# Half of the four copies that place a turned attention tile are issued by GpSimd instead of SyncE

## The chip, the cores and the metric

The kernel runs on one core of a Trainium2 chip. The metric is the device time of one execution in microseconds (us). Before the change the median of three runs is 8271.41 us, the runs lie between 8253.08 and 8294.09 us.

The engines of the core are TensorE (PE in the profile, its weight loads PEld), VectorE (DVE), ScalarE (ACT), GpSimd (POOL) and SyncE (SP). SyncE computes nothing; it issues most of the transfers. SPq and POOLq are the sequencers that issue a transfer.

## The reference, cut to what matters

```python
# x: (4, 128, 64, 64) float32
x = x + deform_conv3x3(group_norm(x))          # layer 0: offsets and mask from a conv, bilinear gather
t = to_tokens(x)                               # (4, 4096, 128)
u = ln(t)
qkv = qz_ring(u.reshape(4, 4096, 16, 8) + rx)  # 16 heads of 8: cosines and their running products
s = einsum('bhsd,bhtd->bhst', q, q) / sqrt(8)  # q, k and v are the same tensor
ctx = einsum('bhst,bhtd->bhsd', softmax(s), q)
x1 = ln(u + ctx @ w_comb.T + b_comb)
t = t + ln(x1 + relu(cos(x1[..., :8]) * cos(ry) @ w1.T + b1) @ w2.T + b2)
t = t + moe_top2_of_8(ln(t))
out = from_tokens(t)
```

The attention carries most of the time: four batches, 16 heads, 4096 positions each. Queries and keys are the same tensor, so the matrix of scores of a head is symmetric, and so is its exponential. A block of exponentials that has been computed for the query chunk `sc` and the key tile `t` serves a second time, turned round, with `t` as the queries and `sc` as the keys.

## The kernel before, in words

**The attention loop.** The main loop (from L1499) goes over `steps`. A step is one key tile `t` of 128 positions for one run; a run is a batch, a group of four heads and a query chunk `sc` of 512 positions. `scores` (L1323) makes four matmuls (L1331) and two exponentials of 128x1024 on ScalarE (L1340), which give the tiles `e`. `context` (L1344) multiplies them with the values `qf` into the accumulator `acc` (L1354). The scores run up to two steps (`LAG`) ahead of the context.

**The turned tiles.** For some steps (`gives`) the block of exponentials is used a second time. `turn` (L1200) does it in three stages:

1. VectorE transposes the two `e` tiles in blocks of 32x32 into a tile `st` of 128x2048 floats (L1210, two instructions).
2. `move` (L1218) takes a tile `et` and issues four transfers (L1222). Copy `r` reads partitions 32r to 32r+31 of `st` (8 KB in each) and writes slot `r` of all 128 partitions of `et` (2 KB in each): 256 KB a copy, 1 MB a turned tile.
3. `from_turned` (L1268) makes 32 matmuls of TensorE (L1277) from `et` and the values `vt` into `acc`, in two halves of 16. It needs all four copies.

There are 704 turned tiles, so 2816 copies. Two `st` buffers (`NST`) and three `et` buffers (`NET`) are in use by turns. An `st` is free when its four copies have read it; an `et` is free when TensorE has used it.

**What sets the order.** The order of the instructions on TensorE, VectorE, SyncE and GpSimd is the order of the program text, which a planner, the class `Beside` (L65), works out as the program is written. Each engine then carries out its own list in order, and waits where a semaphore isn't there yet. The planner keeps an estimate of time for TensorE (`now`), VectorE (`dve`) and GpSimd (`pool`). Jobs beside the attention (the preparation of the next batch, the feed forward and the experts of a finished chunk, the turned tiles) are slotted in when the planner holds them ready. `later(when, emit)` writes an instruction down once the planned time `when` is past; the copies of a turned tile are written at the planned end of its transposes (L1228), or when an `et` comes free (L1234 to L1245). The matmuls of a turned tile are planned at 6.0 us after the copies (L1226).

**SyncE's list.** It holds, besides the copies of the turned tiles, nearly all other transfers: keys and values (L1302, L1304), queries (L1312, L1316), the store of a run's context (L1178), the transfers of the preparation (L729, L762, L882, L883) and of the layers behind the attention.

**GpSimd's list.** It holds the 1152 indirect gathers of the deformable convolution (`gather`, L650; three to a unit of work, up to two units ahead), 132 small powers that give the reciprocal standard deviation of the norms (`rsqrt`, L410 to L417), and 32 copies of the features (L859). The planner books a unit's three gathers with 3.9 us on `pool` and their landing 2.8 us later (`gathered`, L197), and a power with 1.1 us (`powered`, L202). The gathers end with the preparation of the last batch.

Of the kernel before, what the change touches and what calls it, by code (L numbers as in the profile page):

```python
# [229 lines left out]
def ve(n, ops=1):  # L230

    return ops * (0.17 + n / 960.0)
# [12 lines left out]
def kernel(  # L245
# [22 lines left out]
    nc = tc.nc  # L268
# [12 lines left out]
    beside = Beside()  # L281
# [918 lines left out]
    def turn(es, run, t):  # L1200
        b, g, sc = runs[run][:3]
        while len(unsent) >= NST:
            beside.flush()
            if len(unsent) >= NST:
                beside.pull("turned")
        unsent.append(run)
        st = work.tile([P, 4, 4, P], F32, tag="st", name=f"st{run}_{t}", bufs=NST)
        beside.dve = max(beside.dve, beside.now + 0.9)
        for pr in range(2):
            nc.vector.transpose(  # L1210
                out=st[:, :, 2 * pr : 2 * pr + 2, :].rearrange("p o h (q j) -> p o (h q) j", j=32),
                in_=es[pr].rearrange("p h (q o i) -> p o (h q) i", o=4, i=32),
            )
            beside.dve += ve(1024)

        outstanding[run] += 1

        def move():  # L1218
            unsent.remove(run)
            e = work.tile([P, 4, 4, P], F32, tag="et", name=f"et{run}_{t}", bufs=NET)  # L1220
            for r in range(4):
                nc.sync.dma_start(  # L1222
                    out=e[:, r].rearrange("p h x -> p (h x)"),
                    in_=st[32 * r : 32 * (r + 1)].rearrange("p o h x -> p (o h x)"),
                )
            beside.add("turned", from_turned(run, t, e, beside.now + 6.0), -1)  # L1226

        beside.later(beside.dve, lambda: granted(move))  # L1228
# [5 lines left out]
    def granted(emit):  # L1234
        if room[0]:
            room[0] -= 1
            emit()
        else:
            asking.append(emit)
# [28 lines left out]
    def from_turned(run, t, e, landed):  # L1268

        b, _, sc = runs[run][:3]  # L1270
        kt = t % 4
        part = 1 + gifts[b][sc].index(t // 4)
        for half in range(2):
            yield need(pe=MM256, hold=None, after=landed)
            for q in (2 * half, 2 * half + 1):
                for h in range(4):
                    nc.tensor.matmul(  # L1277
                        accs[run][32 * h : 32 * (h + 1), P * kt : P * (kt + 1)],
                        lhsT=window(q, h, part),
                        rhs=e[:, :, h, 32 * q : 32 * (q + 1)],  # L1280
                        start=False, stop=False,
                    )
        outstanding[run] -= 1
        beside.later(beside.now + 0.9, returned)
# [363 lines left out]
```

## Time and profile before

| | |
|---|---|
| median of three runs | 8271.41 us (8253.08 to 8294.09) |
| the profiled execution | 8280.98 us, its span 8279.2 us |
| mean granted clock of TensorE | 0.932 of full speed |
| TensorE busy | 7100.3 us, 86% of the span |
| ScalarE busy | 6385.2 us, 77% |
| VectorE busy | 5251.0 us, 63% |
| GpSimd busy | 1630.9 us, 20% |
| copies of turned tiles (L1222), all on SyncE | 2816 |
| first and last of them | 966.2 us, 7986.3 us |
| gathers on GpSimd (L650) | 1152, the last at 6055.5 us |

All lines that are quoted come from one profiled execution. An engine is busy while one of its computing instructions runs; the issue of a transfer isn't counted. A group of instructions in the profile is given by its line, engine, operation and tiles (written<-read), then its count, then busy time and mean duration, then the idle time of the engine just before those instructions, with what ended most of it. A line of the waits names the waiting instruction, the one that it waited for, then the total in us, the number of waits and the longest one. The chain of waits is followed back from the last instruction: each step goes to what released it.

### The profile page before, as it was taken

The numbers are of one execution on the slowest core, as the hardware profiler recorded it, in microseconds if no ns is written. First come the engines' busy times: TensorE is split into PE (matmuls) and PEld (weight loads), VectorE is DVE, ScalarE is ACT, GpSimd is POOL, SyncE is SP. The second block draws the span as 40 slices with busy tenths as digits, with TensorE's granted clock in tenths as the row PEclk, the third lists the DMA queues.
The fourth block names the chain that finished last, engine by engine and source line by source line (L and its number), as shares of the span: only waits on it lengthen the run. The fifth ranks groups of instructions, "written<-read, shape, count | busy, mean of one in ns | idle before, by whom it ended". The sixth has DMA issues, their size and how long they took to land.

```text
span 8279.2 us, 196502 instructions
## 1 busy us (share of the span) xinstructions
PE 7100.3 (86%) x79896; PEld 2614.4 (32%) x79896; DVE 5251.0 (63%) x9904; ACT 6385.2 (77%) x6825; POOL 1630.9 (20%) x1327
## 2 busy tenths in 40 slices
PE   3689898989998888889898888888899998898996
PEld 2122232222333333333333333333333333333332
DVE  7666366664555777767565776666665665666555
ACT  0579898879887778778687877777788887787894
POOL 5443043421002313213000322122200000000000
PEclk6789999999999999999899999999999999999998
DMA  6777478785567788887757888887775777778641
GB/s 180 214 216 203 132 231 221 222 227 141 142 168 203 203 222 232 221 231 202 189 142 187 251 229 234 226 216 210 206 187 138 176 202 188 196 197 210 176 119 38
DMA packets 1051268, 1598.91 MB, mean 193 GB/s; under 512 B 188994, under 2 KB 418012, under 8 KB 1050364
## 3 DMA queue, kind: packets, MB, share of 16 engines
q1 hardware_dynamic: 950654, 1280.06, 59.7%
q0 software_dynamic: 92160, 302.06, 11.9%
q8 instruction: 630, 10.32, 0.5%
q10 hardware_dynamic: 7550, 4.22, 0.2%
q14 instruction: 274, 2.24, 0.1%
HBM read 612.82 MB, written 234.90 MB: 102 GB/s over the span
## 4 chain that ended last, share of the span: by engine, by line
PE 47%; DMA 23%; SPq 13%; DVE 11%; issue 4%; ACT 1%; POOL 1%; ACTq 0%; DVEq 0%; POOLq 0%
PE acc L1354 21%; DMA et<-st 17%; PE sc L1331 12%; SPq L1222 9%; PE acc L1277 6%; DVE st L1210 4%; PE conv_ps L301 2%; PE e_ps L301 2%; DVE v L670 1%; DMA sT<-smd 1%; SPq L729 1%; PE f_ps L301 1%; ACT e L1340 1%; DMA v<-tab,idx 1%; DMA smd<-tr 1%
## 5 line engine op out<-in xcount | busy, mean ns | idle before, releaser
L1340 ACT ACTIVATE e<-sc 128x1024 f32<-128x1024 f32 x6784 | 6379.0, 1058 | 1723.4 <-PE sc L1331 1512.2
L1354 PE MATMUL acc<-e,qf 128*9 128x512 f32 (+1 forms) x26368 | 3583.2, 615 | 31.8 <-DVE cu L1568 22.4
L1331 PE MATMUL sc<-qT,kT 32*128 32x512 f32 x13568 | 2136.3, 506 | 127.1 <-ACT e L1340 42.9
L1210 DVE STREAM_TRANSPOSE st<-e 128x1024 f32<-128x1024 f32 x1408 | 1666.2, 1222 | 910.2 <-DMA et<-st 633.1
L1331 PEld LDWEIGHTS sc<-qT,kT 32*128 32x128 f32 x13568 | 857.1, 186 | 3336.2 <-ACT e L1340 2822.6
L650 POOL DMA_INDIRECT v<-tab,idx x1152 | 1434.3, 1245 | 1907.5 <-DVE tr L717 1385.5
L1277 PE MATMUL acc<-et,vt 128*32 128x128 f32 x22528 | 970.4, 294 | 716.3 <-DMA et<-st 693.6
L1277 PEld LDWEIGHTS acc<-et,vt 128*32 128x32 f32 x22528 | 580.6, 115 | 1086.1 <-issue 951.2
L1354 PEld LDWEIGHTS acc<-e,qf 128*9 128x9 f32 (+1 forms) x26368 | 626.8, 93 | 566.6 <-issue 311.1
L415 POOL TENSOR_TENSOR r<-ln_t,expo 128x4 f32<-128x4 f32 x96 | 110.5, 1151 | 3246.0 <-DVE ln_t L413 3166.1
L670 DVE TENSOR_TENSOR v<-v,wt 128x1536 f32<-128x1536 f32 x384 | 666.5, 1736 | 103.4 <-DMA v<-tab,idx 103.3
L675 DVE TENSOR_TENSOR v<-v 128x768 f32<-128x768 f32 x384 | 366.7, 955 | 8.0
L717 DVE STREAM_TRANSPOSE tr<-v 128x128 f32<-128x128 f32 x1080 | 248.7, 281 | 188.8 <-DMA smd<-tr 182.5
L301 PE MATMUL conv_ps<-sT,wconv_sb 128*32 128x256 f32 x4320 | 353.9, 401 | 0.0
L1105 DVE TENSOR_TENSOR eo<-e_ps,gt 128x512 f32<-128x512 f32 x256 | 173.5, 680 | 271.3 <-PE e_ps L301 269.2
L1566 DVE COPY cu<-acc 128x512 f32<-128x512 f32 x128 | 88.3, 690 | 225.3 <-PE acc L1354 225.2
L676 DVE TENSOR_TENSOR v<-v 128x384 f32<-128x384 f32 x384 | 215.5, 561 | 13.3
L1259 DVE COPY vt<-own 128x144 f32<-128x144 f32 x96 | 22.7, 236 | 268.8 <-PE acc L1277 268.7
L859 POOL COPY fx<-rn 128x512 f32<-128x512 f32 x32 | 28.0, 874 | 765.5 <-DVE rn L858 487.4
L301 PE MATMUL f_ps<-w_sb,h 128*32 128x128 f32 x4096 | 169.1, 285 | 0.0
L415 POOL TENSOR_TENSOR rstd<-lt_t,expo 128x4 f32<-128x4 f32 x32 | 53.5, 1673 | 510.0 <-DVE lt_t L413 439.0
L301 PEld LDWEIGHTS conv_ps<-sT,wconv_sb 128*32 128x32 f32 x4320 | 105.6, 112 | 93.4 <-issue 89.6
(232 smaller groups left out, 3440.5 us busy)
## 6 DMA issues: line engine op xcount, KB each, us to landing
et<-st SPq DMA_DIRECT2D x2816, 256.0 KB
kT<-kTd SPq DMA_DIRECT2D x333, 256.0 KB
smd<-tr SPq DMA_DIRECT2D x360, 192.0 KB
sT<-smd SPq DMA_DIRECT2D x360, 192.0 KB
qT<-qTd SPq DMA_DIRECT2D x166, 256.0 KB
atd<-cu SPq DMA_DIRECT2D x128, 256.0 KB
qf<-fqd SPq DMA_DIRECT2D x333, 72.0 KB
aT<-atd SPq DMA_DIRECT2D x76, 256.0 KB
```

What stands on the lines that cost most here:

```text
L301: nc.tensor.matmul(dst[c : c + 32], lhsT=lhsT[:, c : c + 32], rhs=rhs, start=start, stop=stop)
L650: nc.gpsimd.indirect_dma_start(out=v[:, k, :], out_offset=None, in_=tab, in_offset=bass.IndirectOffsetOnAxis(ap=idx[:, j, kk : kk + 1], ax ...
L670: nc.vector.tensor_tensor(v4, v4, w12[:, :, None].to_broadcast([P, 12, C]), ALU.mult)
L675: nc.vector.tensor_tensor(v[:, :, : 2 * C], v[:, :, : 2 * C], v[:, :, 2 * C :], ALU.add)
L676: nc.vector.tensor_tensor(v[:, :, :C], v[:, :, :C], v[:, :, C : 2 * C], ALU.add)
L717: nc.vector.transpose(out=tr9[:, k, :, j % 4, :], in_=v[:, k, :C].rearrange("p (c i) -> p c i", i=32),)
L1210: nc.vector.transpose(out=st[:, :, 2 * pr : 2 * pr + 2, :].rearrange("p o h (q j) -> p o (h q) j", j=32), in_=es[pr].rearrange("p h (q o i ...
L1222: nc.sync.dma_start(out=e[:, r].rearrange("p h x -> p (h x)"), in_=st[32 * r : 32 * (r + 1)].rearrange("p o h x -> p (o h x)"),)
L1277: nc.tensor.matmul(accs[run][32 * h : 32 * (h + 1), P * kt : P * (kt + 1)], lhsT=window(q, h, part), rhs=e[:, :, h, 32 * q : 32 * (q + 1)] ...
L1331: nc.tensor.matmul(ps[i // 2][:, i % 2, :], lhsT=kT[h : h + 32, P * (t % 4) : P * (t % 4 + 1)], rhs=qT[h : h + 32, :], start=True, stop=True,)
L1340: nc.scalar.activation(e, ps[pr], AF.Exp, scale=1.0 / math.sqrt(HD))
L1354: nc.tensor.matmul(acc[32 * h : 32 * h + width, :], lhsT=lhsT, rhs=es[h // 2][:, h % 2, :], start=(t == ts[0]), stop=(t == ts[-1]),)
```

## The change

`move` writes the same four copies. Copies 0 and 1, which read partitions 0 to 63 of `st`, stay on SyncE; copies 2 and 3, which read partitions 64 to 127, go to GpSimd. They are written in the order 0, 2, 1, 3, and the planner books 2.2 us on its estimate for GpSimd for each turned tile. Nothing else is touched; source, destination and size of each copy stay.

```diff
         def move():
             unsent.remove(run)
             e = work.tile([P, 4, 4, P], F32, tag="et", name=f"et{run}_{t}", bufs=NET)
-            for r in range(4):
-                nc.sync.dma_start(
+            beside.pool = max(beside.pool, beside.now) + 2.2
+            for r in (0, 2, 1, 3):
+                (nc.gpsimd if r > 1 else nc.sync).dma_start(
                     out=e[:, r].rearrange("p h x -> p (h x)"),
                     in_=st[32 * r : 32 * (r + 1)].rearrange("p o h x -> p (o h x)"),
                 )
```

## The prediction

> **What bounds the kernel now.** I read the page's busy times first, then its chain of waits, then the groups, then the waits of TensorE and of SyncE's queue, and last the chain piece by piece.
>
> ```profile
> PE 47%; DMA 23%; SPq 13%; DVE 11%; issue 4%; ACT 1%; POOL 1%; ACTq 0%; DVEq 0%; POOLq 0%
> PE acc L1354 21%; DMA et<-st 17%; PE sc L1331 12%; SPq L1222 9%; PE acc L1277 6%; DVE st L1210 4%; PE conv_ps L301 2%; PE e_ps L301 2%; DVE v L670 1%; DMA sT<-smd 1%; SPq L729 1%; PE f_ps L301 1%; ACT e L1340 1%; DMA v<-tab,idx 1%; DMA smd<-tr 1%
> ...
> L1210 DVE STREAM_TRANSPOSE st<-e 128x1024 f32<-128x1024 f32 x1408 | 1666.2, 1222 | 910.2 <-DMA et<-st 633.1
> ...
> L650 POOL DMA_INDIRECT v<-tab,idx x1152 | 1434.3, 1245 | 1907.5 <-DVE tr L717 1385.5
> L1277 PE MATMUL acc<-et,vt 128*32 128x128 f32 x22528 | 970.4, 294 | 716.3 <-DMA et<-st 693.6
> ```
>
> The way of a turned tile holds a quarter of the chain: its copies' flight 17%, their issue by SyncE 9%. The chain also runs where TensorE has other work, so these 26% aren't the gain. What the copies cost is TensorE's idle time: 716.3 us ahead of L1277, 693.6 of them ended by a copy's landing. TensorE is idle for 1161 us in all (gaps between its matmuls, added up); most of the other 445 us lies ahead of the first turned tile and in the tail. So the copies are the one large wait of the bottleneck engine, and 716 us is the most that mending them can save. VectorE, too, waits 633.1 us for copies to have read an `st`.
>
> The last piece shows one tile:
>
> ```profile
> 6627.28 0.23 SPq L1222
> 6627.51 0.04 issue
> 6627.55 1.18 SPq L1222
> 6628.73 0.04 issue
> 6628.78 0.91 SPq L1222
> 6629.69 0.04 issue
> 6629.73 6.27 DMA et<-st
> 6636.00 0.14 issue
> 6636.14 0.65 PE acc L1277 x16
> ```
>
> Issue after issue on SyncE, then the flight, then the matmuls at once. The records of all 704 tiles say the same: the four issues take 0.63, 0.85, 1.21 and 1.41 us in the mean (4.1 us, 2816 of them 2884 us of SyncE's time); later ones take longer[...]. From the first issue to the last landing pass 8.17 us in the median (7.4 to 9.95 for eight in ten), 8.48 in the mean. In 393 tiles the matmuls begin within 0.4 us of the landing. From the transposes' end to the first issue pass 0.07 us in the median, 1.36 in the mean; the copies then stand behind others on SyncE:
>
> ```profile
> SPq L1178 <- DVE cu L1566: 859.5, 99, 41.8
> SPq L1222 <- DVE st L1210: 609.1, 326, 8.9
> SPq L1304 <- PE acc L1354: 265.5, 80, 8.4
> ```
>
> **SyncE's part.** It loses 1408 issues. Its two copies no longer stand behind two others: 0.63 + 0.85 = 1.5 us of issue, and in the few tiles with nothing else on the queues the second copy landed some 5.3 us after the first issue, with two more behind it. I put SyncE's half at 5 to 6 us. SyncE also gains 1408 x 1.3 us (the mean of the third and fourth) = 1.8 ms of free time, so L1302, L1304 and L1312 come earlier; they are no large wait of TensorE (36 and 34 us for keys and queries, in the opening), so I count nothing. SyncE's half still stands behind L1178 and L1304 as before.
>
> **GpSimd's part.** No plain transfer of GpSimd is in the trace. The nearest row is its gather, also 256 KB in 128 rows: 1.245 us each in the mean (0.94 to 2.53), 0.30 us between two. Two copies: 2 x 1.25 + 0.3 = 2.8 us. Is GpSimd free? At the transposes' end it is at work in 8% of the tiles, and the stretch of work before it gets to a new entry is 0.37 us in the mean. Then the flight: from a gather's issue to its landing pass 4.85 us in the median (at least 2.13), but those read HBM in three at a time; SyncE's fourth copy lands 3.84 us after its issue in the median, 3.5 for the quickest quarter, with three copies ahead of it in its queue. GpSimd's has one, so I take 3.5. Its half lands 0.37 + 2.8 + 3.5 = 6.7 us after the transposes. That is the later half: the tile lands 8.48 - 6.7 = 1.8 us sooner. Bounds: with 4.85 us of flight 8.0, so 0.2 to 0.5 sooner than today's median and mean; with 0.94 us an issue, no hold and 2.13 us of flight SyncE's half is the later one at some 5.3, so 3.2 sooner.
>
> **What 1.8 us is worth.** I go through TensorE's 327 waits ahead of L1277 (median 1.3 us, a tenth over 5.2) and cut each by the lead: 1.0 us sooner saves 275 us, 1.5 saves 362, 2.0 saves 425, 2.5 saves 475, 3.2 some 530. For 1.8 us: 400 us. Next late is TensorE's own work: between 970 and 8000 us it is busy 6186 of 7030 us, ScalarE 5603, so 400 us fit under both.
>
> [...] The rows:
>
> ```profile
> core 0: us, PE busy (x) PEld busy (x) DVE busy (x) ACT busy (x) POOL busy (x), PEclk, DMA share, GB/s
> 1495.00:1505.00 10.00, 10.00 (x114) 3.77 (x110) 2.80 (x3) 5.79 (x7) 0.71 (x1) 0.74 0.99 320
> 6624.00:6634.00 10.00, 10.00 (x124) 3.60 (x124) 7.79 (x9) 8.77 (x10) 0.00 (x0) 1.00 0.91 216
> ```
>
> A stretch of turned copies alone moves 216 GB/s with the DMA engines 91% taken; one in which gathers of GpSimd and transfers of SyncE (turned copies among them) fly together moves 320. So the engines aren't spent at 216. In the few quiet tiles the first packet of a tile starts 1.2 us after the first issue, the last one 5.7 us later, and the landing follows within 0.5: 7.4 in all. [...] By the 320 row 1.05 MB takes 3.3 us, the bytes are ready at 5.0, and GpSimd's 6.7 stands. [...]
>
> **What is given back.** GpSimd's busy time grows by 704 x 2.5 = 1760 us, from 20% to 43%. Behind its copies stand gathers and powers. Until 6100 us some 480 tiles take 480 x 2.8 = 1340 of 5130 us, 26%; an entry that comes then waits 1.4 us, 0.36 us over all. 384 units of gathers, of which 51 are waited for today: 18 to 140 us on VectorE, I take 20. 132 powers: 48 us on VectorE, I take 20. VectorE isn't the bound (4519 of 7030 us), so on TensorE this is less, but the copies' waits for `et` (18 us on SyncE for L1277) now hold GpSimd's list too: 20. Together 60 us; bounds 0 (VectorE's slack covers all) and 190. The planner's 2.2 us shift jobs to other steps: sign unknown, 40 us either way. A gather waiting for VectorE's L717 (1385.5 us, 165 times) could hold copies behind it, but both lists follow VectorE's order, so the copies' own transposes come later than what the gather waits for; nothing.
>
> **The sum.** 8281 (profiled execution; its span 8279 and 2 us around it) - 400 + 60 = 7941; the median of the runs is 10 us lower: 7930.
>
> **Rivals.**
>
> [...]
>
> No change: the copies come sooner and TensorE waits for something else. For it: VectorE waits 910 us ahead of L1210, of which 235 for ScalarE. Against: no other wait of TensorE exceeds 83 us. 8271.
>
> Slower: GpSimd's half becomes the late one. 224 of the 1152 gathers took over 1.6 us, up to 2.53. [...] It decides from the point where GpSimd's half takes 8.48: 1.5 us an issue at 4.85 us of flight, 2.2 us at 3.5. [...]
>
> **Chances.** Main case 0.60 (7740 to 8060: 530 us saved and nothing given back, to 275 saved and 60 given back), small gain 0.18, no change 0.08, slower 0.14. The range 7740 to 8270 leaves out the slower case and part of no change. Half a per cent, 41 us, is about what a measurement of this kernel tells from nothing. Faster 0.78, same 0.08, slower 0.14.
>
> **What would show it.** Right: the idle time ahead of L1277 falls from 716 to some 320 us; VectorE's wait of 633 us for copies falls by half or more; L1222 on SyncE takes under 0.9 us a copy; GpSimd's copies take 0.95 to 1.3 us; TensorE's busy time stays near 7100. Wrong: GpSimd's copies take over 1.5 us, or L1277 waits mostly for GpSimd's half, or SyncE's issues stay at 1 us each (then bytes were the limit), or new waits of VectorE for gathers and powers exceed 150 us.

## The result, and the profile after the change

| | before | after |
|---|---|---|
| median of four runs on one chip | 8263.67 us (8253.08 to 8294.09) | 8538.10 us (8524.42 to 8557.20) |
| the profiled execution, its span | 8280.98 us, 8279.2 us | 8542.64 us, 8540.9 us |
| mean granted clock of TensorE | 0.932 | 0.919 |

The ratio is 1.0328, with a 95% interval of 1.0292 to 1.0363: the changed kernel is slower by 3.3%. The median of before is one of four runs here, one more than in the table ahead. From L1222 on, every line number in the changed kernel is higher by one (the copies are L1223, the turned matmuls L1278).

The page after, its busy times, its two large DMA queues (packets, MB, share of 16 engines) and the groups that answer to those shown of before:

```profile
PE 7154.3 (84%) x79896; PEld 2625.5 (31%) x79896; DVE 5262.0 (62%) x9904; ACT 6384.6 (75%) x6825; POOL 2400.1 (28%) x2735
...
q1 hardware_dynamic: 747902, 910.87, 39.3%
q0 software_dynamic: 204800, 671.25, 29.1%
...
L1210 DVE STREAM_TRANSPOSE st<-e 128x1024 f32<-128x1024 f32 x1408 | 1665.9, 1221 | 936.7 <-DMA et<-st 648.7
L1223 POOL DMA_DIRECT2D et<-st x1408 | 788.2, 567 | 4310.2 <-PE sc L1332 1077.5
...
L1278 PE MATMUL acc<-et,vt 128*32 128x128 f32 x22528 | 968.4, 294 | 812.0 <-DMA et<-st 803.8
```

The move was made: 1408 copies, 369 MB, went from queue q1 to q0. GpSimd's 2400 us of busy time hold 788 us of their issues: unlike SyncE's, the profile counts GpSimd's issues as busy. TensorE's wait ahead of the turned matmuls, which was to fall from 716 to about 320 us, rose to 812 us. VectorE's wait for copies that have read an `st` did not halve either (633 before, 649 now). The page's chain of waits breaks off here after 7% of the span, so I do not use it.

The view of the tile `et` gives the issues (ns: least, median, most):

```profile
L1223 SPq DMA_DIRECT2D et<-st x1408: 542/602/4946, 969.1 to 8165.0; - x176
L1223 POOL DMA_DIRECT2D et<-st x1408: 536/556/924, 969.3 to 8165.4; - x176
```

GpSimd issues a copy in 0.56 us, where 1.25 was expected. SyncE's median fell from 0.95 us (L1222 before: 542/946/3617) to 0.60, but only because the third and the fourth copy are gone from it: copies 0 and 1 take 0.77 and 1.00 us in the mean, for 0.63 and 0.85 before. From the records of all 704 turned tiles, in us:

| | before | after |
|---|---|---|
| transposes' end to first issue of either queue, mean | 1.36 | 0.24 |
| transposes' end to SyncE's first issue, mean | 1.36 | 1.33 |
| transposes' end to GpSimd's first issue, mean | | 0.65 |
| first issue to last landing, median / mean | 8.17 / 8.48 | 8.74 / 9.71 |
| transposes' end to last landing, median / mean | 8.71 / 9.84 | 8.91 / 9.95 |
| SyncE's half: transposes' end to landing, mean | | 9.80 |
| GpSimd's half: the same, mean | | 8.47 |
| keys (`kT`), SyncE: issue to landing, mean | 4.47 | 6.02 |
| `smd`, SyncE: the same | 5.11 | 6.53 |
| gathers, GpSimd: the same | 6.09 | 6.79 |

SyncE's pair leaves no sooner than before, GpSimd's pair leaves early, and the tile arrives no earlier. SyncE's half is the later one in 71% of the tiles. The keys, `smd` and the gathers, which fly beside the copies, take longer as well.

Where the 262 us of span went is seen by cutting the span at the last exponential (8175.43 us before, 8357.42 after): 182 us ahead of it, 80 us behind. The stretch behind it, first of the kernel before, then after (columns: stretch, length, busy times with instructions, granted clock, DMA share, GB/s):

```profile
8175.43:8279.20 103.77, 42.07 (x490) 23.76 (x486) 62.91 (x178) 0.46 (x2) 3.02 (x3) 0.64 0.09 25
```

```profile
8357.42:8540.90 183.48, 79.42 (x946) 44.22 (x938) 116.93 (x322) 0.46 (x2) 6.04 (x6) 0.65 0.09 26
```

The work in it has nearly doubled (946 matmuls for 490): the planner has left one more piece of feed forward and experts behind the attention, where TensorE has nothing else to do. Ahead of the cut, TensorE was idle 166 us longer (1270 us, 1104 before) and busy 17 us longer. Over the whole span its idle time grew from 1161 to 1369 us, and the same number of matmuls was busy 54 us longer, at a granted clock of 0.919 in place of 0.932.

The edit therefore has two suspects, which can be taken apart: the planner's 2.2 us, and the second queue.

### The profile page after: what moved, and what is told of

Same layout as the page of the kernel before. It is cut to its first block, busy times and chain, and to the rows that moved or that the text cites. A ratio compares the mean times of both kernels' runs of the same rounds, so it can differ in the third digit from the quotient of the medians.

```text
span 8540.9 us, 198988 instructions
## 1 busy us (share of the span) xinstructions
PE 7154.3 (84%) x79896; PEld 2625.5 (31%) x79896; DVE 5262.0 (62%) x9904; ACT 6384.6 (75%) x6825; POOL 2400.1 (28%) x2735
## 5 line engine op out<-in xcount | busy, mean ns | idle before, releaser
L1223 POOL DMA_DIRECT2D et<-st x1408 | 788.2, 567 | 4310.2 <-PE sc L1332 1077.5
L1278 PE MATMUL acc<-et,vt 128*32 128x128 f32 x22528 | 968.4, 294 | 812.0 <-DMA et<-st 803.8
L650 POOL DMA_INDIRECT v<-tab,idx x1152 | 1414.4, 1228 | 633.3 <-issue 286.8
L1278 PEld LDWEIGHTS acc<-et,vt 128*32 128x32 f32 x22528 | 580.3, 115 | 1180.8 <-issue 1140.5
L670 DVE TENSOR_TENSOR v<-v,wt 128x1536 f32<-128x1536 f32 x384 | 667.0, 1737 | 164.9 <-DMA v<-tab,idx 164.6
L986 DVE TENSOR_SCALAR h<-h_ps,b_sb 128x512 f32<-128x512 f32 x128 | 93.3, 733 | 73.4 <-PE h_ps L984 72.8
```

Source lines behind the costliest of these rows:

```text
L650: nc.gpsimd.indirect_dma_start(out=v[:, k, :], out_offset=None, in_=tab, in_offset=bass.IndirectOffsetOnAxis(ap=idx[:, j, kk : kk + 1], ax ...
L670: nc.vector.tensor_tensor(v4, v4, w12[:, :, None].to_broadcast([P, 12, C]), ALU.mult)
L1223: (nc.gpsimd if r > 1 else nc.sync).dma_start(out=e[:, r].rearrange("p h x -> p (h x)"), in_=st[32 * r : 32 * (r + 1)].rearrange("p o h x ...
L1278: nc.tensor.matmul(accs[run][32 * h : 32 * (h + 1), P * kt : P * (kt + 1)], lhsT=window(q, h, part), rhs=e[:, :, h, 32 * q : 32 * (q + 1)] ...
```

## The experiments

The kernels ran in four groups, each on a chip of its own with the kernel before beside it: e1 to e4 (before 8383.90 us), e5 to e8 (8267.93), e9 to e11 (8367.81) and e12 to e15 (8267.40). So there are two kinds of chips here, one at some 8268 us and one at 8368 to 8384. Since they differ by over 1%, kernels are compared by their ratios to before within a group, each given with its 95% interval. A ratio is that of the means of the runs without a profile; the times in us are medians of all runs, so their quotient can differ from it by 0.3%.

**The two parts of the edit, alone.** `e1_book_only` keeps the copies as they were and adds only the planner's line; `e2_queue_only` moves the copies and leaves that line out.

```diff
 e1: +            beside.pool = max(beside.pool, beside.now) + 2.2
 e2: -            for r in range(4):
     -                nc.sync.dma_start(
     +            for r in (0, 2, 1, 3):
     +                (nc.gpsimd if r > 1 else nc.sync).dma_start(
```

> All four copies stay on SyncE in their old order; only the planner books 2.2 us for GpSimd per turned tile. Theory A (the booking re-orders the jobs on TensorE, VectorE and SyncE, and that order is the worse one): slower than before by most of the 270 us, 8430 to 8550 us. Theory B (the transfers or GpSimd's list are what costs): within 60 us of before, 8220 to 8330 us.

> Copies 2 and 3 go to GpSimd, without the booking: TensorE, VectorE and ScalarE have the same lists as before the change. Theory A: within 60 us of before, 8220 to 8330 us, since a tile lands no sooner from two queues. Theory B: 8430 to 8550 us. My prediction's step (a tile lands sooner, TensorE waits 400 us less) would give 7870 us; the changed kernel's trace already speaks against it.

Measured: e1 8462.02 us, 1.0091 (1.0061 to 1.0121); e2 8621.03 us, 1.0258 (1.0214 to 1.0302). The product, 1.035, is the whole change within its interval. Each of the two theories on record had it all in one part: e1 lies between them, e2 where theory B had it. The stretch behind the last exponential, e1 and then e2:

```profile
8260.48:8447.20 186.72, 81.29 (x946) 45.89 (x938) 117.13 (x322) 0.46 (x2) 6.04 (x6) 0.64 0.09 26
```

```profile
8526.20:8629.90 103.70, 42.40 (x490) 24.00 (x486) 62.92 (x178) 0.46 (x3) 3.02 (x3) 0.64 0.08 25
```

The booking alone makes the longer tail, 83 us more than before, and its 0.91% (78 us) are no more than that. It moves no copy; it tells the planner that GpSimd is taken, and a job slips past the end. The queue alone leaves the lists of TensorE, VectorE and ScalarE as they were, the tail too, and costs 2.6%. So the second queue, not an order of work, is the larger part.

**Which copies go?** `e3_order_only` stays on SyncE and takes the reordered loop alone: low and high halves of `st` by turns. `e4_odd_on_pool` sends the odd copies to GpSimd, so that each queue reads both halves.

```diff
 e3: -            for r in range(4):
     +            for r in (0, 2, 1, 3):
 e4: -                nc.sync.dma_start(
     +                (nc.gpsimd if r % 2 else nc.sync).dma_start(
```

> All four copies on SyncE, in the order 0, 2, 1, 3, no booking. If reading low and high partitions by turns lets more bytes through in one queue, a tile lands up to 1 us sooner and the time falls by 100 to 250 us (8010 to 8160). If the order of the copies doesn't matter: within 40 us of before, 8220 to 8310 us.

> Copies 1 and 3 go to GpSimd, 0 and 2 stay on SyncE, no booking: each queue has a copy of the low and one of the high partitions. If the split by partition halves matters, this differs from the queue-only kernel by over 60 us (slower, as both queues then read the same half at once). If bytes and packets alone matter: within 40 us of the queue-only kernel.

Measured: e3 8195.82 us, 0.9767 (0.9736 to 0.9799); e4 8581.24 us, 1.0237 (1.0196 to 1.0278). With an even split over two queues, which halves each queue reads makes no difference that these runs can tell. With one queue the order matters a good deal: in e3 nothing changes but the order of four issues, and 2.3% go.

**Is it GpSimd's list, or its bytes?** `e8_small_on_pool` leaves the four copies on SyncE and gives GpSimd two further transfers a tile of 1 KB each into a scratch tile, which wait for the same transposes: the waiting for the transposes and the issuing, with almost none of the bytes. The wait for a free `et`, which the real copies have too, is not in it. `e5_before_again` is the unchanged kernel.

```diff
 e8: +            for r in (2, 3):
     +                d = work.tile([32, 8], F32, tag="dm", name=f"dm{run}_{t}_{r}", bufs=8)
     +                nc.gpsimd.dma_start(out=d, in_=st[32 * r : 32 * (r + 1), 3, 3, :8])
```

> All four copies on SyncE in the old order, and two further transfers on GpSimd per turned tile, which wait for the same transposes but move 1 KB each to a scratch tile that nothing reads. Theory L: slower by most of the 2.6% of the queue-only kernel. Theory S: within 0.5% of before.

> The kernel before, unchanged, once with a profile, as the measure for the others of this call on the same chip: the time of before on this chip within 0.3%; L1277 waits some 700 us for copies, a tile lands 8.2 us after its first issue in the median.

Measured: e8 8300.67 us, 1.0034 (1.0021 to 1.0047), e5 8266.47 against 8267.93. The group of the added transfers in e8, then that of the real copies on GpSimd in e2:

```profile
L1228 POOL DMA_DIRECT2D dm<-st x1408 | 717.1, 514 | 4240.3 <-DVE st L1210 3653.8 <-DVE ln_st L816 75.3 <-DVE zf L392 51.9
```

```profile
L1222 POOL DMA_DIRECT2D et<-st x1408 | 787.4, 567 | 4430.5 <-DVE st L1210 1129.5 <-PE sc L1331 973.5 <-issue 792.8
```

GpSimd issues as often as with the real copies and is idle about as long ahead of the issues (4240 us for 4431, though the profile names other releasers for much of it), for 0.34%, some 28 us. That leaves over 2% of e2's 2.6% for what happens to the bytes once they fly from two queues.

**How many copies, and one queue or two?** The four kernels below send one, three or four copies to GpSimd, without the booking.

```diff
 e7:  (nc.gpsimd if r > 2 else nc.sync), order 0, 1, 2, 3
 e11: (nc.gpsimd if r else nc.sync),     order 0, 2, 1, 3
 e6:  nc.gpsimd,                         order 0, 2, 1, 3
 e9:  nc.gpsimd,                         order 0, 1, 2, 3
```

> All four copies on GpSimd, in the order 0, 2, 1, 3, no booking; the lists of TensorE and VectorE as before. Theory S (bytes are the limit, and a second queue only lets the copies and SyncE's other transfers slow each other): GpSimd's first bytes start 1 us later than SyncE's, everything of SyncE's shares with them, so at least as slow as the queue-only kernel, 2.5 to 5% over before. Theory L (the copies' waits in GpSimd's list hold up gathers and powers): 2.5% over before, as with two copies. If only the split of one tile over two queues hurts: within 1% of before.

> Only copy 3 on GpSimd, 0 to 2 on SyncE in the old order, no booking. Theory S: less of the bytes on the second queue, about half of the loss, 1 to 1.7% over before. Theory L: one waiting entry holds the list as long as two, 2 to 2.7% over before. My prediction's step would have it faster.

> All four copies on GpSimd in the order 0, 1, 2, 3, no booking; only the order differs from the kernel with all on GpSimd in the order 0, 2, 1, 3, which was at 1.002 of before. Theory P (two copies in a row that read the same half of the partitions slow each other, in whatever queue): a quiet tile lands 0.2 to 0.6 us later than with the other order (6.8 us), and the time is 1.5 to 3% over before. If the order matters on SyncE's queue alone: within 0.5% of the other order, 0.997 to 1.007.

> Copy 0 on SyncE, copies 2, 1, 3 on GpSimd, no booking. Theory U (sharing a tile evenly between two queues lets the 16 DMA engines drift apart, and the tile waits for the last): an uneven split drifts less than 2 to 2, a quiet tile lands at 6.8 to 7.2 us, and the time is 0.985 to 1.01 of before. If every byte on the second queue costs the same: 1.03 and more.

The time went:

| copies on GpSimd | kernel | us | before beside it | ratio |
|---|---|---|---|---|
| none, order 0, 2, 1, 3 | e3 | 8195.82 | 8383.90 | 0.9767 (0.9736 to 0.9799) |
| one | e7 | 8186.08 | 8267.93 | 0.9905 (0.9881 to 0.9928) |
| two, low and high half | e2 | 8621.03 | 8383.90 | 1.0258 (1.0214 to 1.0302) |
| two, even and odd | e4 | 8581.24 | 8383.90 | 1.0237 (1.0196 to 1.0278) |
| three | e11 | 8571.86 | 8367.81 | 1.0233 (1.0200 to 1.0266) |
| four, order 0, 2, 1, 3 | e6 | 8284.51 | 8267.93 | 1.0017 (1.0002 to 1.0032) |
| four, in order | e9 | 8610.89 | 8367.81 | 1.0270 (1.0239 to 1.0300) |

If GpSimd's queue were poor as such, the cost would grow with the copies on it. It doesn't: one copy gains, two and three cost the same, and all four cost almost nothing in the better order. The kernels with one queue make a square of four: on SyncE the order is worth -2.3%, on GpSimd -2.5%; in either order the move of all four from SyncE to GpSimd costs 2.6 to 2.7%. So two things seem to be at work, and to add. Of the theories on record, S and L both had e6 at 2.5% or more and e7 slower than before, and U had e11 at 1.01 at most: all three missed. That only the split hurts, named third for e6, fits e6 and not e9. P had e9 at 1.5 to 3%, and came true.

The table has a weak point. The order on SyncE was measured on both kinds of chips (e3 and e10 at 8384 and 8368 us, e15 at 8267), but the kernels with one copy on GpSimd, or all four by turns, ran only where before takes 8268 us, and those with two, three, or four in order only where it takes 8368 or more. e13 and e14 below were to try the other kind of chip and fell on the same one, so the rival that their expectations name stays untested. For the even split there is the changed kernel itself, which ran where before takes 8264 us: its 182 us ahead of the tail are 2.2%. For the rest the traces speak against the rival: TensorE's idle time hardly hangs on the chip in the order-only kernel (1027, 1039 and 1008 us in e3, e10 and e15; what differs is its busy time, 7155, 7142 and 7062 us), while it is 1313 us with four copies in order (e9) against 1154 by turns (e13), and 1332 with three (e11) against 1106 with one (e7).

**The best version again, and profiles of three corners of the square on one chip.**

> The order-only kernel once more (all on SyncE, 0, 2, 1, 3), to set it beside the others on one chip: 0.973 to 0.981 of before if its gain doesn't hang on the chip.

> The kernel before with a profile on this chip, as the measure for the next three: within 0.3% of the runs of before beside it, TensorE idle some 1150 us, a quiet tile at 7.5 us.

> All four copies on GpSimd in the order 0, 2, 1, 3 once more, beside the order-only kernel on one chip. Theory P (copies in a row that read the same half slow each other in any queue; the two orders on GpSimd stood at 1.002 and 1.027, but on different chips): 0.98 to 1.005 of before, 2% or more below the other order on GpSimd. If the chip made that difference: 1.02 to 1.03 where before takes 8370 us, 1.00 where it takes 8270.

> Copy 3 alone on GpSimd once more. Theory P: the copy of the high half runs beside those of the low half, so faster than before on any chip, 0.975 to 0.995. If the gain was the chip's: 1.00 or more on the other chip.

> The order-only kernel on the chip of this call: 0.973 to 0.981 of before where before takes 8370 us; where before takes 8270 us, 0.985 to 0.995 if the chips differ only in what the old order costs.

Measured: e10 0.9767 (0.9739 to 0.9796), e13 1.0025 (1.0011 to 1.0038), e14 0.9911 (0.9881 to 0.9940), e15 8080.25 us (8069.26 to 8089.00) against 8267.40, 0.9770 (0.9744 to 0.9797). The order alone beats the kernel before by 2.3%, on three chips, and the changed kernel by more. The page's rows of the queues and of the turned matmuls, first in the kernel before (e12), then in e15:

```profile
q1 hardware_dynamic: 950654, 1280.06, 59.7%
q0 software_dynamic: 92160, 302.06, 12.0%
...
L1277 PE MATMUL acc<-et,vt 128*32 128x128 f32 x22528 | 971.3, 295 | 695.3 <-DMA et<-st 678.6
```

```profile
q1 hardware_dynamic: 950654, 1280.06, 57.7%
...
L1277 PE MATMUL acc<-et,vt 128*32 128x128 f32 x22528 | 961.7, 293 | 569.8 <-DMA et<-st 546.3
```

The span is 192 us shorter: TensorE is idle for 136 us less and busy for 55 us less, at a granted clock of 0.935 for 0.931. The same packets and bytes take less of the DMA engines' time: those of 1 KB and more, of all queues, add up to 5132 us an engine, not 5418. Copies 0 and 1 read the same half of the partitions, and so do 2 and 3; taken by turns, two neighbours in the queue never read the same half. In tiles with nothing else on the queues (8 of 704 in e15, 6 or 7 in the kernel before) a tile's packets take 4.2 us an engine in place of 4.7 to 4.8, and over all tiles the last copy lands 8.00 us (mean) after the first issue in place of 8.48, and the gain is the turned tile's own: the keys and `smd` land no sooner (4.48 us before and 4.62 in e15, 5.26 and 5.38). Why neighbours that read the same half cost more is not shown; the gain by order is measured.

The waits of e13 (all on GpSimd), then of e12 beside it (total, times, longest):

```profile
PE acc L1277 <- DMA et<-st: 621.1, 294, 7.7
...
DVE tr L717 <- DMA smd<-tr: 247.0, 45, 21.2
...
DVE v L670 <- DMA v<-tab,idx: 156.9, 77, 7.4
```

```profile
PE acc L1277 <- DMA et<-st: 678.6, 303, 13.1
...
DVE tr L717 <- DMA smd<-tr: 190.9, 44, 14.1
...
DVE v L670 <- DMA v<-tab,idx: 111.5, 52, 8.3
```

With all four copies on GpSimd the tile itself lands sooner (9.49 us after the transposes in the mean, 9.82 in e12), and TensorE waits less for it. The transfers that stayed on SyncE pay: keys 5.36 us for 4.48, `smd` 6.99 for 5.26. In this kernel the two come near to cancelling: TensorE is idle for 1154 us, 1144 in e12.

**What two queues do to one tile.** In the traces a landing is sixteen increments of a semaphore: a turned tile with nothing else on the queues has 64 for its four copies, before and after the change. The increments carry no engine, so what each of them stands for is not shown. In tiles with nothing else on the queues (7 each, medians), all four copies on SyncE, the increments of the last copy come within 1.0 us (6.5 to 7.5 us after the first issue). In e2 those of SyncE's second copy come over 3.5 us (4.4 to 7.9). Over the tiles whose increments are all on record (495 to 661 of the 704), the time from the first to the last increment of the last copy is, in the mean, 1.6 us before, 1.8 in order 0, 2, 1, 3, 2.0 with one copy on GpSimd, 2.7 with four, 2.7 to 3.1 with two or three, 3.1 in the changed kernel. Counted from the tile's first issue, the eighth increment of the last copy comes after 7.50 us before and 7.80 in the changed kernel (medians 7.22 and 6.69), the last one after 8.40 and 9.66 (8.10 and 8.74). So half of them are there about as early as before, and the tile waits for the stragglers. The packets' own time isn't what grew: in the tiles with nothing else on the queues it is 4.1 us an engine in the changed kernel (5 tiles), 4.8 before, and the tile still lands at 7.8 us in place of 7.5.

Two more things differ with the queue. In those five tiles GpSimd's first packet comes 2.6 us after the tile's first issue, SyncE's after 1.2. And the packets have another shape: by the counts of q1 and q0 above, a copy is 144 packets from SyncE and 80 from GpSimd. By their sizes in the traces of before and after, q1 has 180224 packets of 2 KB and 22528 of 4 bytes fewer after the change, q0 90112 of 4 KB and 22528 of 4 bytes more; over 1408 copies these are 128 of 2 KB or 64 of 4 KB a copy, and 16 of 4 bytes. No kernel here splits a tile over two queues with equal packets, and ScalarE was not tried as the second issuer. So whether the second queue as such costs, or its packets, or its late start, is not shown.

## Why the prediction was wrong

**"GpSimd's part", the flight: this step failed.** I took 3.5 us from the end of a copy's issue to its landing because GpSimd's second copy has only one ahead of it in its own queue. It measured 6.5 us (median; 7.1 from the start of the issue). The copies of the other queue count as well: in the few tiles with nothing else on the queues (5 to 11 a trace) all four have landed 7.5 us after the first issue before, 7.8 us after, and 7.7 us with all of them on GpSimd in order (e9). The issue term was wrong the other way (0.56 us, not 1.25), so GpSimd's half left early and landed 8.47 us after the transposes, not 6.7. The 1.8 us that the sum was built on, and with them the 400 us, did not exist: transposes' end to landing went from 9.84 to 9.95.

**A slip in the same sum.** The 8.48 us from which 6.7 was taken is counted from the first issue, and the 6.7 from the transposes' end, where today's figure is 9.84. SyncE's half, at 5 to 6 us from its first issue, comes at 6.4 to 7.4 with the 1.36 us ahead of it. In its own terms the prediction should have had the tile 2.5 to 3.1 us sooner; the measured flight takes that away too.

**"SyncE's part": failed for the same reason.** Its half was put at 5 to 6 us from its first issue and came after 8.47 us (mean; 8.28 median). Its issues took 1.8 us for the 1.5 expected, and it stood behind L1178 and the others as long as before, as said (1.33 us). I had read the 3.84 us of the fourth copy, with three ahead of it, as what a queue of four costs; with two in each queue, SyncE's two landed as late after their first issue as the four had done (8.48). That SyncE's other transfers were put at nothing missed that some fly longer: the keys by 1.5 us.

**The 320 GB/s row.** I took from it that the DMA engines weren't spent at 216 GB/s, and let GpSimd's 6.7 us stand. That row had gathers from HBM in it; it was no second reader of `st`, and its DMA share of 0.99, like the 0.91 of the other row, said that the DMA engines were all but taken. The even split gained nothing and cost 2.4 to 2.6% (e4, e2). The small gain, 0.18 of the chances, was on the wrong side too: no run with two of the four copies on GpSimd shows one. The gain lay elsewhere, in the order of the halves within one queue.

**"What is given back", 60 us: of the right order.** GpSimd's list and issues cost some 28 us (e8). VectorE's idle time ahead of L670, which waits for the gathers, rose from 103 to 165 us (132 in e2), three times the 20 that I took and inside the 140 that I allowed. GpSimd's busy time grew by 769 us, not 1760. None of this decides anything.

**The planner's 2.2 us, "sign unknown, 40 us either way": mis-sized.** No working stood behind the 40 us. It measured 78 us: one more piece of work moved behind the last exponential, where TensorE has nothing else to do.

**The slower rival** had the side but not the mechanism: it needed issues of 1.5 us or more on GpSimd and GpSimd's half as the late one. Issues took 0.56 us, and that half is the late one in 29% of the tiles.

**What stays open.** Why the landings spread when two queues feed the DMA engines was not settled; the spread itself is shown, and the packets' shape and GpSimd's later start stand as rivals. How e2's 2.6% divide between stragglers and the longer flights of keys, `smd` and gathers isn't shown either; both came together. Nor is it shown why one copy on GpSimd gains 0.9%, or that it does so on the other kind of chip. The spread alone doesn't rank the kernels: e6 has 2.7 us of it and costs 0.2%.

## What to carry to other kernels

When several transfers of one tile are waited for together, ask first how long their bytes keep the DMA engines busy: where that was most of the time from issue to landing, as here (4.8 of 7.5 us in the tiles with nothing else on the queues), a second issuer with half of the transfers brought the tile in no sooner (9.95 us after the transposes for 9.84), and other transfers flew longer (keys 6.02 us for 4.47). Before moving transfers to another queue, try their order in the one that they have, with neighbours that read different halves of the partitions; here it was worth 2.3% for one edited line. And test a planner's booking apart from the work that it stands for: alone it cost 0.9% here, as one more piece of work fell behind the last exponential.

## What the runs showed of the hardware that was not expected

- GpSimd issues a plain transfer of 256 KB in 0.56 us in the median and 0.92 at most (changed kernel), and the fourth of four in a row takes 0.59 in the mean (e13). SyncE's issues of the same copies take 0.54 to 3.6 us before the change: 0.63, 0.85, 1.21 and 1.41 in the mean for the first to the fourth of a tile. In the 41 tiles before which SyncE had issued nothing for 5 us they take 0.54, 0.69, 1.23 and 1.55, so there they grow with the tile's own copies ahead.
- Here copies that followed each other in a queue and read the same half of the partitions took more of the DMA engines' time than by turns: in the 7 to 15 tiles with nothing else on the queues 4.8 us a tile and engine for 4.2 on SyncE (before, e15), 4.8 for 4.0 on GpSimd (e9, e13).
- With copies of one tile on two queues the sixteen increments of the last landing come 3.1 us apart in the mean, where it is 1.6 with one queue (changed kernel, before).
- The same 256 KB copy is 128 packets of 2 KB in the trace of before, where SyncE issues it, and 64 of 4 KB in that of the changed kernel where GpSimd does, with 16 of 4 bytes either way.
